# Self attentions of levels 0 and 2 issued in the program's own order on each engine

## The chip, the cores and the metric

The kernel runs on one core of a Trainium2 chip. A core has a matrix engine (PE, whose weight loads are listed apart as PEld), a vector engine (DVE), an activation engine (ACT), a general engine (POOL, also called GpSimd) and a queue that issues DMAs (SP). Each has its own list of instructions and works through it in order; engines wait for one another by semaphores. The time is the device time of one execution in microseconds, and the number quoted for a kernel is the median of its runs. A profile is one more execution, and its span runs from the first instruction to the last.

## What is computed

A four-level "perceiver": on each level a cross attention to a context, a self attention and a feed-forward layer, each added to the stream `x` after a layer norm. `x` has 64 sequences of 32 tokens with 256 features, so 2048 tokens. Two of the twelve layers matter here:

```python
# level 0: 16 heads of 16, q and k normed by their own root mean square
q = rms_norm(proj(Wq), qn_w)
k = rms_norm(proj(Wk), kn_w)
v = proj(Wv)
scores = jnp.einsum('bhnd,bhmd->bhnm', q, k) * scale
attn = jax.nn.softmax(scores, axis=-1)
out = jnp.einsum('bhnm,bhmd->bhnd', attn, v)
return out.transpose(0, 2, 1, 3).reshape(B, N, D) @ Wo.T

# level 2: 16 heads of 64, a second layer norm for q alone, q and k of unit length,
# two learned null keys and values, a distance bias and a causal mask
q = (xn @ Wq).reshape(b, n, h, dh).transpose(0, 2, 1, 3)
kv = x @ Wkv
k = jnp.concatenate([nk, k], axis=2)
v = jnp.concatenate([nv, v], axis=2)
q = _l2norm(q) * q_scale
k = _l2norm(k) * k_scale
sim = jnp.einsum('bhid,bhjd->bhij', q, k) * SCALE
sim = sim + slopes * bias
sim = jnp.where(causal[None, None], -neg, sim)
attn = jax.nn.softmax(sim, axis=-1)
out = jnp.einsum('bhij,bhjd->bhid', attn, v)
return out.transpose(0, 2, 1, 3).reshape(b, n, h * dh) @ Wout
```

The sum over the twelve layers is `x = x + layer(_layernorm(x))` in each case, in float32 throughout.

## The kernel before

`x` stays in SBUF as 16 tiles of 128 tokens (4 sequences of 32 tokens each), and each layer is one method that works through these tiles. The method is traced into a program, a sequence of instructions each of which names its engine. A scheduler of the framework then sets the order in which each engine issues them: it takes instructions whose inputs are there by its own estimate of times, by priority, and gives out tile buffers as they come free. So the order in which the program is written is a wish, and the trace shows the order that came of it. `NT` is 16.

Both self attentions are written as software pipelines. A tile's work is cut into steps (small functions), and iteration `i` of the loop lists steps of several tiles, so that one tile's waits can lie beside another's work.

Level 0, method `l0_attn`, iteration `i`, in the order of the list `steps`: `projected(i)` (PE: values into the bank `m`, then q and k together into `qk`; ACT: copy of the values, then the square of q and k; DVE: its sums `ms`, lines L809 and L810), `norm_1(i+1)` (DVE statistics, POOL rsqrt L391 and L393), `unit(i-1)` (DVE, L823: q and k times their inverse lengths), `lengths(i, 0)` (POOL, L819: the power -0.5 of half of the 32 sums), `heads_first(i-1)` (PE: four transposes; ACT: three scaled copies, L829 and L833), `scores(i-2)` (PE: 32 small matmuls; DVE: maximum L859 and subtraction L860; ACT: exponential L863), `norm_2(i+1)` (DVE, L789), `weighted(i-3)` (PE: 16 matmuls into bank `o`; ACT: copy `oT`, L886), `turned(i+1)` (PE: two transposes; ACT: copy `nT`, L796), `divided(i-2)` (DVE: sums L512 and reciprocal L516; POOL: product L870), `lengths(i, 1)` (POOL, L819, the other half), `output(i-3)` (PE: projection into bank `o`; DVE: residual add, L892) and `diagonal(i-2)` (DVE: four transposes, L936, which lay the probabilities out in blocks, `bd`, for `weighted` of the next iteration). The PSUM banks: `m` and `o` have one buffer each, `qk` two, the scores four banks.

Level 2, method `l2_attn`, has the same plan with larger heads. Its steps of iteration `i` are, in order: `diagonal(i-2)`, `projected(i, 0)` (q; ACT squares it, L2095), `norm_1(i+1)`, `lengths(i, 0)` (DVE: sums L1992, L1993; POOL: the power, L1995, called `sr`), `weighted(i-2)` (PE, bank `c`; ACT: `oT`, L2180), `norm_2(i+1)` (DVE, L2056 and statistics), `projected(i, 1)` (k), `unit(i, 0)` (DVE, L2105, `qn`), `norm_3(i+1)`, `scores(i-1)` (PE, bank `c`; DVE: bias added, L2140), `lengths(i, 1)`, `exponentials(i-1)` (DVE: L2151 and L2152; ACT: L2153), `output(i-2)` (PE, bank `m`; DVE: residual add, L2187), `unit(i, 1)`, `divided(i-1)` (DVE: L512, L516, L2161; POOL: L2159), `value_rows(i)` (PE, twice bank `m`; ACT: two copies, L2126), `heads_first(i, 0)` (PE, eight transposes; ACT: q, L2117), `turned(i+1)` (PE, four transposes; ACT: `nT`, L2074, and `n2T`, L2078) and `heads_first(i, 1)` (ACT: `kT`, L2112). Banks `m` and `b` (projections and their transposes) have two buffers, `c` one.

All matmuls are written by the helper `mm`, so they carry its line, L438; they are told apart by their tiles. Transposes stand under L2219 and L432.

Of the kernel before, what the change touches and what calls it, by code (L numbers as in the profile page):

```python
# [5 lines left out]


# [2 lines left out]

# [1 line left out]

# [306 lines left out]
class Perceiver:  # L319
# [28 lines left out]
    def forms(self, pool):  # L348

        self.k_qm = self.sb(pool, [128, 2, D + 1 + 64], "k_qm")  # L350
        self.k_tot = self.sb(pool, [128, 1], "k_tot")
        self.k_qa = self.sb(pool, [128, 2 * B], "k_qa")
        self.k_qb = self.sb(pool, [128, 2 * B], "k_qb")

# [405 lines left out]
    def l0_attn(self):  # L762
        nc, tc, a = self.nc, self.tc, self.a
        wqkv = self.weight(a["l0a_wqkv"], 2)
        wo = self.weight(a["l0a_wo"], 4)
        with ExitStack() as st:
# [12 lines left out]
            def norm_1(i):  # L779
                st = self.sb(pool, [128, 6], "ln_st")  # L780
                nc.vector.bn_stats(st, self.x[:, i, :])
                mv = self.sb(pool, [128, 2], "ln_mv")
                nc.vector.bn_aggr(mv, st)
                t_n[i] = mv, self.rsqrt(pool, mv[:, 1:2], LN_EPS, "ln_r")

            def norm_2(i):
                mv, r = t_n[i]
                n = self.sb(pool, [128, D], "n")
                nc.vector.tensor_scalar(n, self.x[:, i, :], mv[:, 0:1], r, ALU.subtract, ALU.mult)  # L789
                t_n[i] = n  # L790

            def turned(i):
                pt = self.sb(ps, [128, 2, 128], "m")
                self.transposed_into(pt, t_n[i], 2)
                nT = self.sb(pool, [128, 2, 128], "nT")
                nc.scalar.copy(nT, pt)  # L796
                t_nT[i] = nT
# [18 lines left out]
            def lengths(i, half):  # L816
                ms, r = t_r[i]
                f = slice(16 * half, 16 * half + 16)
                nc.gpsimd.tensor_tensor(r[:, f], ms[:, f], self.neg_half.to_broadcast([128, 16]), ALU.pow)  # L819
# [72 lines left out]
                nc.vector.tensor_tensor(self.x[:, i, :], self.x[:, i, :], py, ALU.add)  # L892

            norm_1(0), norm_2(0), turned(0)
            for i in range(NT + 3):
                steps = [
                    (i, projected),
                    (i + 1, norm_1),
                    (i - 1, unit),
                    (i, lambda t: lengths(t, 0)),  # L900
                    (i - 1, heads_first),
                    (i - 2, scores),
                    (i + 1, norm_2),
                    (i - 3, weighted),
                    (i + 1, turned),
                    (i - 2, divided),
                    (i, lambda t: lengths(t, 1)),
                    (i - 3, output),
                    (i - 2, diagonal),
                ]  # L910
                for t, step in steps:
                    if 0 <= t < NT and not (t == 0 and step in (norm_1, norm_2, turned)):
                        step(t)
# [1062 lines left out]
    def l2_attn(self):  # L1976
        nc, tc, a = self.nc, self.tc, self.a
        wq, wk, wv = (self.weight(a["l2a_w"][j], 2) for j in range(3))
        wo = self.weight(a["l2a_w"][3], 8)
        with ExitStack() as st:  # L1980
# [65 lines left out]
            def mean_and_scale(src):  # L2046
                st = self.sb(pool, [128, 6], "ln_st")
                nc.vector.bn_stats(st, src)
                mv = self.sb(pool, [128, 2], "ln_mv")
                nc.vector.bn_aggr(mv, st)  # L2050
                return mv, self.rsqrt(pool, mv[:, 1:2], LN_EPS, "ln_r")

            def scaled(src, mr, tag):
                mv, r = mr
                out = self.sb(pool, [128, D], tag)
                nc.vector.tensor_scalar(out, src, mv[:, 0:1], r, ALU.subtract, ALU.mult)  # L2056
                return out

            def norm_1(i):
                t_n[i] = [mean_and_scale(self.x[:, i, :])]  # L2060

            def norm_2(i):
                n = scaled(self.x[:, i, :], t_n[i][0], "n")
                t_n[i] = [n, mean_and_scale(n)]

            def norm_3(i):
                n, mr = t_n[i]
                t_n[i] = [n, scaled(n, mr, "n2")]

            def turned(i):  # L2070
                n, n2 = t_n[i]
                pt = self.transposed(ps, n, "m")
                nT = self.sb(pool, [128, 2, 128], "nT")
                nc.scalar.copy(nT, pt)  # L2074
                pt = self.transposed(ps, n2, "m")
                n2T = self.sb(pool, [128, 2, 128], "n2T")
                for k in range(2):
                    nc.scalar.activation(  # L2078
                        n2T[:, k, :],
                        pt[:, k, :],  # L2080
                        AF.Identity,
                        bias=self.col("L2_attn_norm_b", k),
                        scale=self.col("L2_attn_norm_g", k),
                    )
                t_nT[i] = n2T, nT

            def projected(i, k):
                src, wt = t_nT[i][k], (wq, wk)[k]
                pq = self.sb(ps, [128, 16, 64], "b")
                pf = pq.rearrange("p h d -> p (h d)")  # L2090
                for hf in range(2):
                    f = slice(hf * 512, (hf + 1) * 512)
                    self.mm(pf[:, f], [(src[:, kk, :], wt[:, kk, f]) for kk in range(2)])
                sq = self.sb(pool, [128, 16, 64], "sq")
                nc.scalar.activation(sq, pq, AF.Square)  # L2095
                t_qk[i, k] = pq, sq

            def lengths(i, k):
                pq, sq = t_qk[i, k]
                t_qk[i, k] = pq, norms(sq, 16, 128)  # L2100

            def unit(i, k):
                pq, r = t_qk[i, k]
                t = self.sb(pool, [128, 16, 64], "qn")
                nc.vector.tensor_tensor(t, pq, bcast(r, 2, 64), ALU.mult)  # L2105
                t_qk[i, k] = t.rearrange("p h d -> p (h d)")

            def heads_first(i, k):
                pT = self.transposed_into(self.sb(ps, [128, 8, 128], "b"), t_qk[i, k], 8)
                if k:  # L2110
                    t = kTs[i % 3]
                    nc.scalar.activation(  # L2112
                        t[:, :, :, 2:K], pT.rearrange("p c (b t) -> p c b t", b=NB), AF.Copy, scale=ks
                    )
                else:
                    t = self.sb(pool, [128, 8, 128], "q")
                    nc.scalar.activation(t, pT, AF.Copy, scale=qs)  # L2117
                t_T[i, k] = t
# [69 lines left out]


            norm_1(0), norm_2(0), norm_3(0), turned(0)  # L2190
            for i in range(NT + 2):
                steps = [
                    (i - 2, diagonal),
                    (i, lambda t: projected(t, 0)),
                    (i + 1, norm_1),
                    (i, lambda t: lengths(t, 0)),
                    (i - 2, weighted),
                    (i + 1, norm_2),
                    (i, lambda t: projected(t, 1)),
                    (i, lambda t: unit(t, 0)),  # L2200
                    (i + 1, norm_3),
                    (i - 1, scores),
                    (i, lambda t: lengths(t, 1)),
                    (i - 1, exponentials),
                    (i - 2, output),
                    (i, lambda t: unit(t, 1)),
                    (i - 1, divided),
                    (i, value_rows),
                    (i, lambda t: heads_first(t, 0)),
                    (i + 1, turned),  # L2210
                    (i, lambda t: heads_first(t, 1)),
                ]
                for t, step in steps:
                    if 0 <= t < NT and not (t == 0 and step in (norm_1, norm_2, norm_3, turned)):
                        step(t)
# [290 lines left out]
```

## Time and profile before

Three runs gave a median of 4408.33 us (4405.2 to 4416.82). The profiled execution took 4410.83 us, with a span of 4409.1 us.

| stretch of the span (us) | length | PE busy | DVE busy | ACT busy | POOL busy | granted clock |
|---|---|---|---|---|---|---|
| whole span | 4409.1 | 3824.0 | 1883.8 | 1180.9 | 1165.2 | 0.929 |
| level 0 self attention, 384.5 to 637.4 | 252.9 | 164.19 | 124.08 | 57.23 | 128.31 | 0.72 |
| level 2 self attention, 2411.7 to 2823.5 | 411.8 | 349.74 | 210.96 | 130.17 | 134.44 | 0.97 |

The page cuts the span into 40 slices of 110 us and gives each engine's busy share in tenths (9 is 90% or more), and below it the clock that PE was granted, in tenths of full speed:

```profile
PE   7998662879898596989998888899999999999996
DVE  5554544244344605666655555300000344444335
ACT  2333210123332022333332333201111233333331
POOL 5434531033311135444443333100000211112102
PEclk9998765989999697999999999999999999999997
```

The level 0 attention lies in slices 4 to 6, the level 2 attention in slices 22 to 26. "Busy" for PE is a modelled figure: the ends of matmuls are not measured but computed, so distances between their starts say more. The chain of waits, a second view, follows the work that ended last back to what released it; on this profile it can be followed from the end of the span back through level 2, but not as far as level 0, for which the timeline is used. In a timeline line the first number is the start in us, the second the length, then engine, line, operation, output<-inputs and shapes, and in brackets how long the engine had stood idle and who ended that. DMAs play no part in either loop: their share there is 0.03.

### The profile page before, as it was taken

What the parts mean: (1) busy time and instruction counts of PE and PEld (TensorE: products, weight loads), DVE (VectorE), ACT (ScalarE), POOL (GpSimd) and SP (SyncE); (2) the same over time, 40 slices, a digit from 0 to 9 for tenths busy, and PEclk for the clock granted to TensorE, in tenths of its full rate; (3) what the DMA queues carried; (4) which work ended last, traced back from release to release, by engine and by line L of the source; (5) the groups of instructions that cost most, each with busy time, mean ns of one, the idle gap of its engine ahead of it and who ended that gap; (6) DMA issues with size and microseconds to landing.
All of it is one profiled execution on the core that took longest, in us unless ns stands there. A gap on an engine that the chain in (4) does not pass through costs nothing.

```text
span 4409.1 us, 68941 instructions
## 1 busy us (share of the span) xinstructions
PE 3824.0 (87%) x27148; PEld 2666.7 (60%) x27148; DVE 1883.8 (43%) x5262; ACT 1180.9 (27%) x3175; POOL 1165.2 (26%) x1622
## 2 busy tenths in 40 slices
PE   7998662879898596989998888899999999999996
PEld 6785441556676364767675455444444677777774
DVE  5554544244344605666655555300000344444335
ACT  2333210123332022333332333201111233333331
POOL 5434531033311135444443333100000211112102
PEclk9998765989999697999999999999999999999997
DMA  6441022175000143222221000200001111110000
GB/s 217 132 151 35 1 94 74 44 226 175 3 2 21 57 116 115 73 75 71 76 76 51 1 1 1 81 0 0 0 0 38 38 33 33 33 33 22 2 2 22
DMA packets 162996, 245.25 MB, mean 56 GB/s; under 512 B 27521, under 2 KB 105745, under 8 KB 158449
## 3 DMA queue, kind: packets, MB, share of 16 engines
q1 hardware_dynamic: 152370, 224.92, 16.3%
q0 software_dynamic: 5280, 10.82, 1.1%
q10 hardware_dynamic: 5024, 5.11, 0.3%
q8 instruction: 215, 3.52, 0.3%
q14 instruction: 107, 0.88, 0.1%
HBM read 223.80 MB, written 16.99 MB: 55 GB/s over the span
## 4 chain that ended last, share of the span: by engine, by line
PE 43%; DVE 8%; POOL 6%; ACT 3%; issue 2%; DMA 1%; DVEq 0%; ACTq 0%; POOLq 0%
PE m L438 20%; PE h L438 13%; PE s L438 4%; POOL sr L1995 2%; PE b L438 1%; PE e L2395 1%; ACT e L2382 1%; DVE t L2410 1%; PE m L1944 1%; DVE bd L936 1%; POOL cT L1899 1%; DVE qn L2105 1%; DVE ss L1992 1%; POOL p L1938 1%; DMA cT<-in_ctxT 1%
## 5 line engine op out<-in xcount | busy, mean ns | idle before, releaser
L438 PE MATMUL m<-w,oT 128*128 128x256 f32 x1216 | 293.7, 394 | 11.9 <-DVE oT L1447 4.0
L438 PEld LDWEIGHTS m<-w,oT 128*128 128x128 f32 x1216 | 235.8, 197 | 59.6 <-DVE oT L2340 10.8
L438 PE MATMUL m<-nTg,w 128*128 128x256 f32 x1024 | 231.9, 385 | 1.3 <-ACT nTg L1387 1.1
L438 PE MATMUL h<-h,w 128*128 128x512 f32 x512 | 220.4, 592 | 0.0
L438 PE MATMUL h<-h,h 128*128 128x512 f32 x512 | 220.4, 592 | 0.0
L2271 DVE TENSOR_TENSOR y<-m,row_L_ffn_w_s 128x256 f32<-128x256 f32 x16 | 6.8, 425 | 486.6 <-PE m L438 486.6
L438 PEld LDWEIGHTS m<-nTg,w 128*128 128x128 f32 x1024 | 193.9, 192 | 29.1 <-ACT nTg L1387 1.7
L2382 ACT ACTIVATE e<-s,nm 128x257 f32<-128x257 f32 x256 | 118.2, 474 | 325.3 <-DVE nm L2381 266.5
L438 PE MATMUL s<-cT,ut 128*128 128x257 f32 x768 | 187.4, 390 | 3.6 <-ACT p L1934 2.9
L438 PE MATMUL m<-pT,cn 128*128 128x384 f32 x512 | 177.3, 489 | 0.0
L1938 POOL TENSOR_TENSOR p<-p,rs 128x771 f32<-128x771 f32 x64 | 94.9, 1483 | 299.5 <-DVE rs L1937 195.0
L438 PEld LDWEIGHTS h<-h,w 128*128 128x128 f32 x512 | 97.3, 190 | 122.5 <-issue 122.5
L438 PEld LDWEIGHTS h<-h,h 128*128 128x128 f32 x512 | 97.3, 190 | 122.5 <-issue 122.5
L2272 POOL TENSOR_TENSOR x<-x,y 128x256 f32<-128x256 f32 x16 | 11.9, 744 | 591.6 <-DVE y L2271 591.6
L438 PEld LDWEIGHTS m<-v,eT 128*128 128x128 f32 x1280 | 158.6, 192 | 9.0 <-ACT qT L695 1.8
L438 PEld LDWEIGHTS s<-cT,ut 128*128 128x128 f32 x768 | 144.9, 196 | 27.4 <-issue 4.2
L438 PE MATMUL m<-v,eT 128*128 128x64 f32 x1280 | 158.6, 271 | 1.4 <-DVE eT L2399 0.7
L936 DVE STREAM_TRANSPOSE bd<-hs_p 32x512 f32<-32x512 f32 x192 | 134.9, 703 | 52.1 <-POOL hs_p L930 37.8
L438 PE MATMUL m<-w,nT 128*128 128x512 f32 (+2 forms) x320 | 132.6, 548 | 26.6 <-DVE x L2187 23.2
L2264 ACT ACTIVATE h<-h,cols 128x512 f32<-128x512 f32 x64 | 44.0, 687 | 397.1 <-PE h L438 397.1
L438 PE MATMUL o<-bd,v 128*64 128x128 f32 (+1 forms) x1536 | 96.3, 327 | 58.6 <-DVE bd L936 58.6
L1995 POOL TENSOR_TENSOR sr<-ss,neg_half 128x16 f32<-128x16 f32 (+1 forms) x33 | 93.5, 2833 | 140.1 <-DVE ss L1993 140.1
(618 smaller groups left out, 8194.8 us busy)
## 6 DMA issues: line engine op xcount, KB each, us to landing
ct<-in_ctx SPq DMA_DIRECT2D x192, 256.0 KB
cT<-in_ctxT SPq DMA_DIRECT2D x32, 1028.0 KB
cT<-in_ctxT SPq DMA_DIRECT2D x128, 257.0 KB
ab<-abd SPq DMA_DIRECT2D x64, 257.0 KB
rb<-rd SPq DMA_DIRECT2D x16, 514.0 KB
w_all<-in_l0f_w SPq DMA_DIRECT2D x8, 1024.0 KB
w<-in_l1f_down SPq DMA_DIRECT2D x8, 640.0 KB
extra<-maskd SPq DMA_DIRECT2D x16, 257.0 KB
```

Of the source, the lines that this page charges most:

```text
L438: self.nc.tensor.matmul(out, lhsT=l, rhs=r, start=j == 0, stop=j == last)
L936: self.nc.vector.transpose(bd[q, :, b, :], p[q])
L1899: nc.gpsimd.tensor_tensor(cT, cT, bcast(ab[:, 0, :], 1, 2), ALU.mult)
L1938: nc.gpsimd.tensor_tensor(p, p, bcast(rs, 2, S), ALU.mult)
L1944: nc.tensor.transpose(pp[:, g, :], p[:, g, c * 128 : (c + 1) * 128], self.ident)
L1992: nc.vector.tensor_reduce(ss, sq, AX.X, ALU.add)
L1995: nc.gpsimd.tensor_tensor(r, ss, self.neg_half[:p].to_broadcast([p, nh]), ALU.pow)
L2105: nc.vector.tensor_tensor(t, pq, bcast(r, 2, 64), ALU.mult)
L2264: nc.scalar.activation(h2[:, c, :], pa, AF.Gelu, scale=self.col(name, c))
L2382: nc.scalar.activation(e[:, r, :], pss[r], AF.Exp, bias=nm[:, r : r + 1], accum_out=ss[:, r : r + 1])
L2395: nc.tensor.transpose(pe[:, r, :], e[:, r, c * 128 : (c + 1) * 128], self.ident)
L2410: nc.vector.tensor_tensor(t[q], t[q], po[q, :, j, :], ALU.add)
```

## The change

A context manager is added to the class, and each of the two methods enters it just ahead of its loop; it is left when the method's stack closes, ahead of the pools.

```diff
+    @contextmanager
+    def as_written(self, *engines):
+
+        nc = self.nc
+        block = nc.cur_bb
+        first = block.bb.instructions[-1]
+        yield
+        assert nc.cur_bb is block
+        traced = block.bb.instructions
+        start = next(k for k in reversed(range(len(traced))) if traced[k] is first) + 1
+        engines = [e.engine for e in engines]
+        last = {}
+        for ins in traced[start:]:
+            if ins.engine not in engines:
+                continue
+            if ins.engine in last:
+                self.tc.add_manual_dep(
+                    ins,
+                    last[ins.engine].name,
+                    mybir.DependencyInfo(mybir.DependencyClass.NoSync, mybir.DependencyReason.DATA),
+                    reason="as_written",
+                )
+            last[ins.engine] = ins
...
             norm_1(0), norm_2(0), turned(0)
+            st.enter_context(self.as_written(nc.tensor, nc.vector, nc.scalar, nc.gpsimd))
             for i in range(NT + 3):
...
             norm_1(0), norm_2(0), norm_3(0), turned(0)
+            st.enter_context(self.as_written(nc.tensor, nc.vector, nc.scalar, nc.gpsimd))
             for i in range(NT + 2):
```

On leaving, it walks over the instructions that were traced since it was entered and, for each of PE, DVE, ACT and POOL, ties every instruction to the one that the program has before it on the same engine. The tie is of the class `NoSync`: it binds the scheduler, and no semaphore wait comes of it, since an engine keeps its own order anyway. Instructions from ahead of the loop and of the next layer are not tied and may still be put between them. The set of instructions, their operands, the tiles and their buffer counts are as before.

## The prediction

> **What bounds the kernel now.** The change lives in two loops, so I read those stages and not the page's averages. The windows view gives their length: level 0's self attention runs from 384.5 to 637.4 us of the span (252.9 us, granted clock 0.72), level 2's from 2411.7 to 2823.5 (411.8 us, clock 0.97). Both work on 16 tiles, one after the other in steady state, so the time is 16 periods.
>
> Level 2 first. Its part of the chain of waits, one period (start, length, what):
>
> ```profile
> 2584.66 3.65 PE b L438 x8
> ...
> 2588.38 1.03 ACT sq L2095
> ...
> 2589.44 1.23 DVE ss L1992
> ...
> 2590.95 2.92 POOL sr L1995
> ...
> 2593.89 1.22 DVE qn L2105
> 2595.11 1.13 DVE ss L1992
> ...
> 2597.10 2.92 POOL sr L1995
> 2600.03 1.23 DVE qn L2105
> 2601.26 0.64 DVE s L2152
> ...
> 2602.67 0.73 DVE sh_s L512
> ...
> 2603.82 1.06 POOL p L2159
> ```
>
> After it come four `L936` transposes (2.85 us), 0.99 us of PE work on `c`, and the next `b`: 24.24 us, through five engines. No engine is full; the loop is a ring of waits. The timeline shows where PE stands still in it:
>
> ```profile
> 2578.04 1.98 PE L438 MATMUL m<-w,nT 128*128 128x512 f32 x4 [1.66 <-DVE x L2187]
> 2583.67 0.40 PE L438 MATMUL c<-bd,v 128*64 128x128 f32 x2 [1.46 <-DVE bd L936]
> ```
>
> The second line is the ring's joint: two matmuls of `weighted(i-2)` were issued ahead of `projected(i, 0)`, so all of PE waits for the transposes. The first follows from DVE doing `unit` (`L2105`) before `L2152` and the residual add `L2187`, whose PSUM bank the second half of `value_rows` wants.
>
> Level 0, timeline of one period (13.7 us):
>
> ```profile
> 480.88 5.78 POOL L819 TENSOR_TENSOR qk_r<-ms,neg_half 128x16 f32<-128x16 f32 x2 [4.37 <-DVE ms L810]
> 486.69 0.69 DVE L823 TENSOR_TENSOR qk<-qk,qk_r 128x512 f32<-128x512 f32 x1 [5.26 <-POOL qk_r L819]
> ...
> 490.39 2.85 DVE L936 STREAM_TRANSPOSE bd<-hs_p 32x512 f32<-32x512 f32 x4 [1.53 <-POOL hs_p L870]
> ```
>
> DVE stands 5.26 us until both `lengths` are done, with the softmax sums and the transposes of other tiles queued behind `unit`; POOL then stands 4.37 us until DVE is through. Here the ring is DVE and POOL alone: transposes 2.85, `ms` to `L810` 1.5, `lengths` 5.8, `unit` to `sh_r` 1.9, POOL's rsqrt and product 1.9. PE is not in it.
>
> **The change, part by part.** It adds no instruction, no copy and no DMA. Inside the two loops each of PE, DVE, ACT and POOL gets the program's order; what is before and after the loops stays free. Method: I wrote every instruction of a loop in a table, per engine in order, each starting when its engine is free and its inputs and buffers are there, with durations from the rows, 0.04 to 0.15 us per hand-over (as between the rows above) and matmuls by their start-to-start distance. With the order that the trace shows, the table gives 24.05 to 24.5 us a period for level 2 (trace 24.24) and 13.0 to 14.7 for level 0 (trace 13.3 to 15.0). So it may be used for the other order.
>
> *Level 2.* In program order `projected(i, 0)` stands ahead of `weighted(i-2)`, so the joint opens: PE no longer waits for the transposes before it starts the next tile. DVE does `L2151`, `L2152` and `L2187` while POOL computes the second `sr` (2.9 us), so the 1.66 us stall goes too. What is late next is PE itself. From the start of `projected(i, 0)`: 3.63, `weighted` 0.92 + 1.68, `projected(i, 1)` 3.63, scores 1.22, output 3.99, values 1.82 + 1.82: 18.71 to the start of `heads_first(i, 0)`. From there the next `projected` waits for ACT, which copies q (1.11), nT (0.36) and n2T (0.82) in that order: in the trace n2T ends 3.16 after that start, plus 0.1. Sum 22.0, of which PE idles about 0.9. Gain 2.27 a period; 13 steady distances make 29.5, the start of the loop 1 to 2, its drain nothing: **-30 us**. The transposes now have 2.9 us of slack before `weighted` needs them; were that cover gone, the old joint would be back at 24.2.
>
> Moved waits: on DVE `sb` (`L2152`) now runs beside POOL's `sr`, a pair the trace does not show. Nearest rows, one for each bound:
>
> ```profile
> 2460.49 1.05 POOL L2159 TENSOR_TENSOR p<-s,sh_r 128x512 f32<-128x512 f32 x1 [3.96 <-DVE ln_mv L2050]
> 2460.64 0.95 DVE L2161 TENSOR_TENSOR p<-s,sh_r 128x32 f32<-128x32 f32 x1
> ...
> 393.55 0.41 DVE L789 TENSOR_SCALAR n<-x,ln_mv,ln_r 128x256 f32<-128x256 f32 x1 [0.70 <-POOL ln_r L393]
> ```
>
> Beside a POOL product, a DVE operation that takes 0.19 elsewhere took 0.95: it ended with POOL. Beside a POOL power (`L393`, running until 394.03), `L789` took its usual 0.41. [...] `L2152` would wait for `sr`'s end, my table then gives 0.8 more a period, and level 2 gains 18 instead of 30. I take the row, since `sr` is a power as `L393` is; 18 stays as the near end. No gain beyond -45: without any idle PE the period is 21.1.
>
> *Level 0.* `lengths(i)` is used one iteration later, so its 5.8 us leave DVE's path altogether: the 5.26 stall goes. But each engine now meets its waits in the written order, and that makes a new ring through PE: `unit` 0.69, `heads_first` 0.60, scores 0.91, max and subtract 1.36, exp 0.63, `oT` copy 0.59, output 1.73, projections 0.86 + 1.88, square 0.60, `ms` 0.86, then `norm_1`'s 0.60, which the program puts ahead of `unit`. Sum 11.3; hand-overs 0.5 more, overlap of neighbours on one engine 0.4 less: 11.5 us if PE runs at full clock. `weighted` (1.9) lies beside max, subtract and exp. PE then idles 2.9 us a period, between the projections and `heads_first`.
>
> The clock decides here. Start-to-start, a 256-column matmul of this stage takes 216 ns at full and 427 at half clock, a 512-column one 429 and 853[...]. 4.75 us of the ring double: 16.2 us at half clock throughout. How the clock was granted (window, PE busy, PEld, DVE, ACT, POOL, then PEclk):
>
> ```profile
> 472.68:476.10 3.42, 1.81 (x69) 1.07 (x68) 2.38 (x7) 1.80 (x4) 2.52 (x6) 1.00 0.02 5
> 476.10:479.51 3.41, 0.06 (x4) 0.07 (x8) 2.90 (x5) 0.00 (x0) 0.41 (x1) 0.50 0.00 0
> 479.51:482.93 3.42, 3.42 (x38) 2.35 (x39) 1.92 (x4) 1.43 (x3) 2.06 (x1) 0.50 0.00 0
> 482.93:486.34 3.41, 3.41 (x15) 2.63 (x14) 0.00 (x0) 0.38 (x2) 3.41 (x2) 1.00 0.00 0
> 486.34:489.76 3.42, 2.22 (x68) 1.06 (x66) 2.17 (x6) 1.81 (x4) 1.52 (x4) 1.00 0.02 5
> ```
>
> The clock changes every 3.41 us. A window with PE half busy (1.81) sends the next to half; 2.22 keeps it; a wholly busy one brings it back. [...] the period 11.5, and the loop takes 203 us in my table against 249 for the order of before: -45. By the rows a window over that gap is under half busy and costs a slow one: the period settles near 13.6 (four windows), the loop at 237 to 245: -8 in the middle. With the threshold moved from half to 0.4 of a window it is -21, to 0.55 -4. I take the rows, and **-10** between these.
>
> At the edges: six tiles of the next stage's statistics (`L419`) fill DVE gaps in level 0 today. If they move behind the loop they cost at most 0.3 us each (1.49 against 1.17 a tile there), 2 us; I count nothing.
>
> **Sum.** Profiled run 4410.83, span 4409.1: -30 - 10 gives a span of 4369 and a run of 4370.8. The profiled run lies 2.5 above the median of 4408.33, so 4368.
>
> **Rivals.**
> A, as above: 4368 (0.70).
> B, the clock stays full in level 0: -30 - 45, 4333 (0.17). [...] Against: the 1.81 row.
> C, level 0 half-clocked throughout: its loop takes 279 in the table, +29, and eats level 2's gain: 4407 (0.04).
> D, the change doesn't do what it says, or another hand-over closes level 2's ring again: 4408 (0.04). Against: PE and DVE orders in the trace do differ from the program's.
> E, slower by the clock: both loops are now paced by PE, so a half clock costs where it cost nothing. It decides from where C is reached and level 2 too drops to half; each such iteration adds 16.8 us of array work (3.55 + 3.55 + 4.0 + 3.4 + 2.3). Two: 4441 (0.05). Against: level 2 shows full clock with PE gaps of 1.7.
>
> **Numbers.** Fewer than 13 us (0.3%) can't be told from nothing. Faster is A and B, 0.87; same C and D, 0.08; slower E, 0.05. The range reaches from B, with level 2 a little better, to level 2 at its near end and level 0 unchanged: 4328 to 4392.
>
> **What would show it.** In level 2: periods of 22.0 between first transposes, `projected(i, 0)` with no wait on `bd`, its only PE wait on `n2T`, `L2152` still 0.72. In level 0: `L819` ahead of `unit` by an iteration, no DVE wait on `qk_r`, periods of 13.6 or 11.5 and the clock beside them. I am wrong if PE waits for `bd` again, if `L2152` stretches, or if level 0 gets longer.

## The result, and the profile after

The changed kernel takes 4346.32 us (median of four runs, 4336.95 to 4352.09) against 4410.96 for the kernel before in the same series: a ratio of 0.985, 95% interval 0.983 to 0.987. The profiled execution took 4348.5 us, its span fell from 4409.1 to 4346.7. Forecast were 4368, so the gain is about 65 us where 40 were expected. Both loops gained:

| stretch | before | after | change |
|---|---|---|---|
| level 0, first `n` to last residual add | 252.9 | 241.4 | -11.5 |
| level 2, first instruction to first transpose (`diagonal`) | 63.9 | 58.7 | -5.2 |
| level 2, first transpose to last residual add | 362.0 | 317.1 | -44.9 |
| all the rest of the span | 3730.3 | 3729.5 | -0.8 |

Level 2, one period. The line numbers are 24 to 26 higher than before. The chain of waits, in order of time (start, length, what):

```profile
2564.41 7.52 PE m L462 x26
...
2572.84 1.11 ACT q L2142
2573.95 0.26 ACT nT L2099
2574.21 0.37 ACT n2T L2103
...
2574.63 3.70 PE b L462 x8
```

Before, this chain went through four engines (PE, ACT, DVE and POOL; the prediction counts five), with POOL's two powers and DVE's sums in it. Now it lies on PE but for 1.8 us in which ACT copies what PE has turned. The timeline shows the one wait that PE has left in the period, and how long the subtraction took that runs beside POOL's power (`sr`, 2566.90 to 2569.81):

```profile
2574.63 3.70 PE L462 MATMUL b<-w,n2T 128*128 128x512 f32 x8 [0.52 <-ACT n2T L2103]
2567.48 0.72 DVE L2177 TENSOR_TENSOR s<-s,mx 128x544 f32<-128x544 f32 x1
```

The waits on `bd` and on the residual add, 1.46 and 1.66 us a period before, are gone. The distance of first transposes is 20.78 us, where it was 24.24.

Level 0, timeline of one period:

```profile
507.87 0.66 DVE L847 TENSOR_TENSOR qk<-qk,qk_r 128x512 f32<-128x512 f32 x1
508.67 0.63 PE L2245 MATMUL m<-ident,qk 128*128 128x128 f32 x4 [3.17 <-DVE qk L847]
```

`unit` (L847) has no bracket: DVE doesn't wait for POOL's powers any more (5.26 us before). In its place PE waits 3.17 us for `unit`, which now stands in DVE's order behind the sums (`ms`) of the next tile, and these come out of PE's own projections by way of ACT's square (L443 is a statistic of the next stage):

```profile
505.60 0.60 ACT L831 ACTIVATE sq<-qk 128x512 f32<-128x512 f32 x1 [1.40 <-PE qk L462]
506.18 0.43 DVE L443 BATCH_NORM_STATS2 ln_st<-x 128x6 f32<-128x256 f32 x1
506.52 0.67 DVE L833 TENSOR_REDUCE ms<-sq 128x32 f32<-128x512 f32 x1
```

In this loop and in that of before the granted clock stands at 1.00 or 0.50, for 3.41 us or a multiple of it. The windows view, cut at these 3.41 us (window, then busy us of PE, PEld, DVE, ACT, POOL, then the granted clock):

```profile
492.45:495.87 3.42, 0.87 (x37) 0.69 (x38) 2.31 (x7) 0.22 (x2) 1.42 (x3) 1.00 0.00 0
495.87:499.28 3.41, 3.23 (x86) 2.13 (x66) 2.23 (x4) 2.23 (x6) 2.25 (x1) 0.50 0.02 5
499.28:502.69 3.41, 3.41 (x8) 2.79 (x9) 0.41 (x2) 0.31 (x1) 2.82 (x2) 0.50 0.00 0
502.69:506.11 3.42, 2.81 (x9) 1.38 (x8) 3.11 (x5) 0.88 (x2) 1.08 (x1) 1.00 0.00 0
```

The window with the wait has PE busy for 0.87 us and the next two run at half clock; then two at full clock, and again. Four windows are 13.66 us, and for the first nine distances (from one tile's first `diagonal` transpose to the next tile's) the loop keeps to 13.4 to 13.8; the next five are 11.1 to 13.1 and the last is 9.7.

### The profile page after: what moved, and what is told of

Read it like the earlier page. It is cut to its first block, busy times and chain, and to the rows that moved or that the text cites. A ratio compares the mean times of both kernels' runs of the same rounds, so it can differ in the third digit from the quotient of the medians.

```text
span 4346.7 us, 68933 instructions
## 1 busy us (share of the span) xinstructions
PE 3818.0 (88%) x27148; PEld 2669.3 (61%) x27148; DVE 1891.4 (44%) x5262; ACT 1181.3 (27%) x3175; POOL 1163.9 (27%) x1622
## 4 chain that ended last, share of the span: by engine, by line
PE 48%; DVE 5%; POOL 3%; ACT 3%; issue 2%; DMA 1%; DVEq 0%; SPq 0%; ACTq 0%; POOLq 0%
PE m L462 23%; PE h L462 13%; PE s L462 4%; PE b L462 3%; PE e L2421 1%; ACT e L2408 1%; DVE t L2436 1%; PE c L462 1%; PE m L1969 1%; POOL p L1963 1%; POOL cT L1924 1%; DMA cT<-in_ctxT 1%; PE o L462 1%; PE m L456 1%; PE y L462 1%
## 5 line engine op out<-in xcount | busy, mean ns | idle before, releaser
L462 PE MATMUL m<-w,oT 128*128 128x256 f32 x1216 | 289.4, 390 | 10.7 <-DVE oT L1472 4.0
L462 PEld LDWEIGHTS m<-pT,cn 128*128 128x128 f32 x512 | 94.8, 190 | 58.5 <-issue 2.4
L462 PE MATMUL m<-cT,w 128*128 128x257 f32 x512 | 130.0, 397 | 0.0
```

The source lines that it names most:

```text
L462: self.nc.tensor.matmul(out, lhsT=l, rhs=r, start=j == 0, stop=j == last)
```

## The experiments

All start from the changed kernel. "Loop" is level 0 from its first `n` to its last residual add, 241.4 us after the change; "level 2" is its first transpose to its last residual add, 317.1 us.

**One loop at a time.** Level 0 without the written order:

```diff
             norm_1(0), norm_2(0), turned(0)
-            st.enter_context(self.as_written(nc.tensor, nc.vector, nc.scalar, nc.gpsimd))
```

> The tie is taken away in level 0 and kept in level 2. If the two loops gain independently of each other (my theory): level 0's loop goes back to about 253 us (periods 13.3 to 15.0), level 2's keeps periods of 20.8, the kernel comes to about 4358, 12 above the changed kernel. If level 0's 12 us came from elsewhere (another execution, a shifted start): its loop stays near 241 and the kernel near 4346.

Measured: 4364.13 us (4359.47 to 4375.15), ratio to before 0.990 (0.988 to 0.991). The loop is 253.4 us with the distances of before, level 2 317.1. The kernel lies 6 us above the 4358 that were expected, the two stages as expected: the two gains are independent, and level 2 has most of it.

**Level 2, PE alone in the written order:**

```diff
             norm_1(0), norm_2(0), norm_3(0), turned(0)
-            st.enter_context(self.as_written(nc.tensor, nc.vector, nc.scalar, nc.gpsimd))
+            st.enter_context(self.as_written(nc.tensor))
```

> In level 2 only PE is tied to the program's order; DVE, ACT and POOL are free as before. Two-rings theory (there are two separate rings of about 24 us, one closed by PE's joint, one by DVE doing unit ahead of the exponentials and the residual add, and each alone keeps the period): my table with PE in program order and the others as before gives 22.7 to 24.4 a period, so nearly the whole gain of level 2 is lost, kernel about 4385 to 4400. Rival, the joint alone (the prediction's main step): 20.8 to 21.5 a period, kernel about 4346 to 4356.

Measured: 4378.67 us in one run; distances of 22.43 us, level 2 338.3. Both readings missed: PE's order alone is worth half of the gain. The wait on `bd` is gone; what is left is the other stall that the prediction showed, in which the second half of `value_rows` waits for the residual add (L2212), now 1.39 us instead of 1.66:

```profile
2604.41 1.98 PE L462 MATMUL m<-w,nT 128*128 128x512 f32 x4 [1.39 <-DVE x L2212]
```

**Level 2, the other three engines in the written order, PE free:**

```diff
-            st.enter_context(self.as_written(nc.tensor, nc.vector, nc.scalar, nc.gpsimd))
+            st.enter_context(self.as_written(nc.vector, nc.scalar, nc.gpsimd))
```

> In level 2 DVE, ACT and POOL are tied, PE is free. Two-rings theory: PE again puts matmuls of weighted ahead of projected and waits for the transposes; table 23.9 to 24.3 a period, kernel about 4390 to 4405. Rival, DVE's order alone makes the gain: 20.8 a period, kernel about 4346.

Measured: 4398.75 us in one run; distances of 23.3 to 26.5, level 2 372.7, 10.7 more than before the change. The timeline of PE shows both reasons:

```profile
2591.12 0.66 PE L462 MATMUL c<-bd,v 128*64 128x128 f32 x2 [2.43 <-DVE bd L961]
...
2592.66 6.09 PE L462 MATMUL b<-w,n2T 128*128 128x512 f32 x8
```

The old joint is back: two matmuls of `weighted`, placed ahead of the projection, wait 2.43 us for the transposes. The stall on the residual add is gone. And the clock is halved here, so that the projection takes 6.09 us instead of 3.70. The windows view around this wait, cut as above:

```profile
2587.27:2590.68 3.41, 1.42 (x13) 1.18 (x11) 2.52 (x4) 3.10 (x5) 0.82 (x1) 1.00 0.00 0
2590.68:2594.09 3.41, 2.97 (x9) 1.53 (x10) 0.90 (x3) 0.00 (x0) 0.79 (x2) 0.50 0.00 0
2594.09:2597.51 3.42, 3.42 (x5) 1.35 (x4) 0.00 (x0) 0.00 (x0) 0.00 (x0) 0.50 0.00 0
```

The twelve distances of the steady part sort themselves by the clock: 23.28 us in the three at full clock throughout, 24.8 to 24.9 with one window at half clock, 26.3 to 26.5 with two. The kernel came into the range of the two-rings theory by luck, then: at full clock its period of 23.9 to 24.3 was too long by 0.6 us or more, and the half clock, which it didn't foresee, made up for it. Against the 24.24 of before, the order of the three engines is worth 0.96 us a period at full clock, PE's order 1.81, both together 3.46. Which of the three engines matters was not tried.

**Level 0, is it the clock?** Three discarded matmuls of 512 columns are put into PE's gap, in the bank that the transposes overwrite; the kernel does more work:

```diff
-                pT = self.transposed_into(self.sb(ps, [128, 4, 128], "m"), t_qk[i], 4)
+                pT = self.sb(ps, [128, 4, 128], "m")
+                for _ in range(3):
+                    self.mm(pT.rearrange("p c t -> p (c t)"), [(wqkv[:, 0, 0:128], wqkv[:, 0, 0:512])])
+                self.transposed_into(pT, t_qk[i], 4)
```

> In level 0 three idle-filling matmuls of 512 columns (2.6 us at full clock) run on PE between the projections and heads_first, into the bank that heads_first then overwrites. Clock theory (period 13.66 is four clock windows, because the gap halves the clock): with the gap filled the clock stays full, the period falls to about 11.5 and level 0's loop from 241 to about 213 us although PE has more to do; kernel about 4318. Rival (the ring of waits sets the period whatever the clock does): 13.7 or longer, since heads_first can only get later; kernel 4346 to 4375.

Measured: 4330.85 us in one run; distances of 11.5 to 11.8 in the steady part, loop 219.9, and the clock full from 430.8 us of the span for 147 us on end. The period is the one expected; the loop is 7 us longer than expected, and it starts at 390.7, with 40 us to go until the clock is full for good. PE's wait for `unit` is 0.23 to 0.50 us from 480 to 520 us, that for `n` 0.91. Against the changed kernel the loop loses 21.5 us by being given more to do. That the half clock came with PE's gap of 3.17 us, and that it held the loop at 13.7, is shown by this.

**Level 0, take the wait away instead.** `unit` of the tile before goes ahead of `projected`:

```diff
                 steps = [
+                    (i - 1, unit),
                     (i, projected),
                     (i + 1, norm_1),
-                    (i - 1, unit),
```

> In level 0's step list, `unit` of the tile before stands ahead of `projected` of this tile, so that VectorE multiplies qk while TensorE is in the projections, and heads_first no longer finds it unfinished; all else as in the changed kernel. Theory (TensorE's gap of 3.2 us before heads_first is what halves the clock, and the half clock is what holds the period at 13.7): with the gap gone the clock stays full and the table gives periods of 9.95 to 10.3 us and a loop of 193 to 195 us in place of 241, the kernel 4300 us (4290 to 4310). Rival (another ring, VectorE's own 9 to 10 us of work in order, or PSUM buffers, sets the pace): periods of 12 to 13.7, the kernel 4330 to 4350.

Measured: 4308.36 us (4298.86 to 4313.84), ratio to before 0.975 (0.973 to 0.977); distances of 10.2 in the steady part, loop 198.5. The windows view, cut as above:

```profile
462.48:465.89 3.41, 1.78 (x84) 1.51 (x88) 3.29 (x9) 1.63 (x4) 0.96 (x2) 1.00 0.02 5
...
482.96:486.37 3.41, 1.90 (x6) 0.62 (x5) 3.34 (x6) 0.97 (x2) 2.24 (x1) 1.00 0.00 0
```

The kernel's time came as expected (the loop 3.5 us above its range), the reason only in part: the gap isn't gone. PE still waits 1.51 us for `unit` and 0.91 for `n`. But from 472.7 us of the span on, the emptiest window of each period has 1.90 us of PE work, and the clock stays full for 85 us on end. One window before that had 1.78: two at half clock follow it, and the one distance of 11.99 among those of 10.2 to 10.5.

**`diagonal` ahead of `output` as well:**

```diff
-                    (i - 3, output),
                     (i - 2, diagonal),
+                    (i - 3, output),
```

> The run with `unit` first, and `diagonal` moved ahead of `output` in the same list, so that the block diagonal of the next tile is not queued on VectorE behind an addition that waits for TensorE. Theory (the periods are then set by VectorE's own work, only the last two tiles are shorter): periods of 10.0, the last two 9.97 and 7.28 in place of 12.1 and 9.75, loop 190, 4 to 5 us below the run with `unit` first alone, 4295 us. Rival: the copies on the block diagonal are hidden and the tail doesn't move: the same time within 2 us.

Measured: 4303.95 us (4297.68 to 4305.80), ratio to before 0.974 (0.972 to 0.976). Of the distances, the first thirteen sum to 135.3 us (135.2 without this step), the last two are 10.50 and 7.59 (10.47 and 9.70): the tail moved, by 2.1 us of the 4 expected, and the loop is 197.1, 1.4 shorter, where 190 was expected. The ranges of the two kernels overlap; they aren't told apart.

**`unit` first, without the written order at level 0.** The step is moved as above, and the line of the change is taken out of `l0_attn`.

> `unit` first as in the run of that name, but level 0's loop is not held to the written order (the line of the change is taken out there, and stays at level 2). Theory (the written order is what makes the position of a step in the list count; the scheduler places by its own times): the loop comes out like that of before, 245 to 255 us, the kernel 4355 to 4368. Rival (the position in the list is all that matters, and the tie is not needed): loop 193 to 200, the kernel 4300.

Measured: 4370.03 us in one run, 2 us above the range; the loop is 253.3, its first thirteen distances within 0.03 us of those before the change. Where the scheduler is free, moving a step in the list bought nothing.

**Level 2, `turned` ahead of the heads:**

```diff
-                    (i, lambda t: heads_first(t, 0)),
                     (i + 1, turned),
+                    (i, lambda t: heads_first(t, 0)),
                     (i, lambda t: heads_first(t, 1)),
```

> In level 2's step list, `turned` of the next tile stands ahead of both halves of heads_first, so that n2T is copied while TensorE turns the heads and the first projection no longer waits for it. The two readings differ in what follows. Theory (the whole list is now a ring through TensorE, and the 0.5 us gap before the first projection is only moved: ScalarE copies nT and n2T ahead of q, so heads_first's second half, scores and the copies behind them come later): level 2's period 21.2 in place of 20.78, the kernel 4353. Rival (the gap is all that TensorE waits for, and taking it away is a plain gain): period 20.3, the kernel 4339.

Measured: 4355.38 us in one run; distances of 21.27, level 2 323.7. PE's 0.52 us of waiting is not a plain gain to be had. In its place PE waits twice for ACT, 0.79 us in all: for the copy of the values, ahead of the second pair of `turned`'s transposes, and for the copy of `q`, ahead of the projection:

```profile
2574.56 0.44 PE L456 MATMUL m<-ident,n 128*128 128x128 f32 x2 [0.46 <-ACT v L2151]
2577.07 3.70 PE L462 MATMUL b<-w,n2T 128*128 128x512 f32 x8 [0.33 <-ACT q L2142]
```

The theory's period came true (21.27 against 21.2), the work that it named as late only in part.

## Why the prediction was right, and where its sizes were off

*Level 2, the mechanism: right.* The joint opened, the stall on the residual add went, and PE sets the pace with its only wait on `n2T`. The PE-only and the others-only runs show that both orders are needed for the whole gain: PE's takes the wait on `bd` away, that of the other three the wait on the residual add, as the step said of DVE. The clearance of the transposes was enough: they end at 2576.06 and `weighted` reads them at 2578.37.

*Level 2, the size: the step that was off.* The sum had 22.0 a period; the trace has 20.78. By PE's start-to-start distances after:

| term of the sum | forecast | measured |
|---|---|---|
| projection of q | 3.63 | 3.53 |
| `weighted` | 0.92 + 1.68 | 2.10 |
| projection of k, scores, output | 3.63 + 1.22 + 3.99 | 3.63 + 1.22 + 3.99 |
| values | 1.82 + 1.82 | 3.43 |
| heads to the next projection | 3.26 | 2.87 |

`weighted` had been priced from two pieces of the trace of before, the first of which had a wait beside it; issued in one piece it takes 0.5 less. And the projection starts when the first half of `n2T` is copied, not both: in the chain above it is 0.37 us of ACT, then 0.04, then PE. These terms are 1.2 us a period, 15.5 us over 13 distances. The start of the loop gave 5.2 us and the first distance 1.5 more, where 1 to 2 had been allowed. "No gain beyond -45" fell for the same reason: it took PE's work as 21.1 a period, from the same split pieces.

*The two sides of the subtraction's price.* The price was right: `L2177` took 0.72 to 0.73 us in each of the 15 tiles in which it lies within POOL's `sr`; the same subtraction in the kernel before (`L2152`), beside no POOL instruction, took 0.71 to 0.73. Neither row of the prediction could have shown this. The DVE product that took 0.95 stood beside a POOL product; `L789`, which kept its 0.41 beside a power, works on one tensor with a mean and a scale per row, and the subtraction on two tensors. Only the run after has the pair. That the subtraction would wait for the end of `sr`, from which the near end of the range was priced, was an assumption that no trace of before showed, and that end wasn't needed.

*Level 0, the mechanism: right; the size, in part by luck.* The wait for `qk_r` went, the new ring goes through PE, the gap is 3.2 us (2.9 forecast), the period is four windows for nine distances, and the loop lost 11.5 us (10 forecast). But the prediction had a period near 13.6 as the steady state. The nine distances together are only 4.7 us shorter than before; the next four, 11.1 to 13.1 where 14.7 to 15.4 stood before, bring 11.2 us, and the last two cost 3.5. And in three more runs with the same instructions in level 0 (PE alone, others alone, `turned` first) this loop took 233.9, 236.8 and 239.5 us, so that its gain is 11.5 to 19.

The prediction's 45 is its table's gain for a clock that stays full, at 11.5 us a period. That a gap of 2.9 us would leave the clock full was an assumption that no trace of before showed; after the change the gap was 3.17, and two windows at half clock followed it (0.50 from 495.87 to 502.69). With the gap filled the period was 11.5 to 11.8, as rival B had it, so B's price was that of something real, only not of this change. The prediction's estimate of 16.2 us for a period at half clock throughout has the scores and `weighted` at one length for both clocks, which made it too short. In the changed kernel they took 1.10 and 1.94 us at half clock (granted from 574.37 to 577.78) and 0.85 and 1.08 at full (from there to 594.85):

```profile
574.95 1.10 PE L462 MATMUL s<-kb,qT 32*32 32x64 f32 x64
575.98 1.94 PE L462 MATMUL o<-bd,v 128*32 128x128 f32 x32
...
586.25 0.85 PE L462 MATMUL s<-kb,qT 32*32 32x64 f32 x64
587.04 1.08 PE L462 MATMUL o<-bd,v 128*32 128x128 f32 x32
```

*The edges: nothing was counted, and the rest of the span changed by 0.8 us; but their place was overlooked.* Six of the next stage's statistics still lie in level 0. All six lie in the ring, one an iteration between the square and its sums (L443 above, 0.43 us each), from 437.7 to 506.2 us of the span. When they are used up the distances fall to 13.50, 13.44 and then 12.02. That the statistics are what keeps the loop at four windows until then was not tried.

*The rivals.* C and D did not come. E's mechanism exists: the others-only run shows a half clock in level 2 (0.50 from 2590.68 to 2597.51) beside waits of 2.43 us, and it ends 10.7 us longer than before. It didn't decide here: PE's wait of 0.52 us a period leaves the clock full for 304 us on end in level 2. The range held the time.

What stays open: why level 0's loop differs among those four runs. It goes with the clock: it stood at half for 125 us of the loop in the changed kernel (241.4), and for 120, 117 and 111 in the runs with 239.5, 236.8 and 233.9. Where the loop starts within a clock window may account for that, as it did in the table of the prediction (237 to 245), but it was not tried.

## What to carry to other kernels

Where a scheduler places the instructions, a hand-built pipeline is only a wish: look for the instruction that was issued ahead of its turn and makes a whole engine wait, and hold all the engines of the ring to the written order, not one: in level 2 the three without PE gained 0.96 us a period at full clock and lost more than that by the half clock that PE's waits brought. With the order held, each place in the list is a decision worth pricing: moving one step made level 0's loop another 43 us shorter (241.4 to 198.5), while the same move bought nothing with the scheduler free. Price a group of instructions from a row in which it runs in one piece, and count PE's work in each of the clock's 3.41 us windows, not only its single waits: in level 0 a window with 0.87 us of it was followed by half clock, and one with 1.90 was not.

The lowest median is that of the changed kernel with `unit` first and `diagonal` ahead of `output`: 4303.95 us, ratio to before 0.974 (0.972 to 0.976); it isn't told apart from `unit` first alone.

## What the runs showed of the hardware

In these loops the clock went with how much PE worked in a 3.41 us window: the one with 0.87 us of PE work (3.17 us wait) was followed by half clock, and so were those with 1.78 (`unit` first) and 1.81 (kernel before), while 1.90 us (`unit` first) kept it full, with waits of 1.51 and 0.91 in each period. The traces show no sharp border in modelled PE work. Two pairs of neighbouring windows from level 0 of the kernel before:

```profile
394.18:397.59 3.41, 1.77 (x5) 0.46 (x3) 0.00 (x0) 0.97 (x2) 3.41 (x3) 1.00 0.00 0
397.59:401.01 3.42, 0.00 (x0) 0.00 (x0) 0.68 (x2) 0.00 (x0) 2.71 (x1) 1.00 0.00 0
...
459.03:462.45 3.42, 1.91 (x70) 1.17 (x70) 2.90 (x9) 1.80 (x4) 1.87 (x4) 1.00 0.02 5
462.45:465.86 3.41, 0.55 (x2) 0.15 (x2) 2.86 (x5) 0.37 (x1) 1.20 (x3) 0.50 0.00 0
```

A window with 1.77 us kept the clock, one with 1.91 lost it. Over the level 0 loops of before and after the windows that lost it had up to 1.91 us, and those that kept it 1.73 (from 588.02 us, after) or more; the run with `turned` first has one that kept it with 1.40 (from 393.42 us). In the loops of before and after both outcomes thus occur only from 0.51 to 0.56 of a window. For the way back no figure comes out: of the changed kernel's windows at half clock, the one with 3.23 us of work shown above did not bring the full clock back, while two others with 3.23 (from 550.48 and from 564.13 us) did; the thirteen wholly busy ones (3.41) in its level 0 loop all did.
